# Turning x1 on VectorE and by transfers in place of TensorE, with a new order inside a chunk

## The chip, the cores and the metric

The kernel runs on one core of a Trainium2 chip, alone. The time is device microseconds (us) of one execution. Engines are named as in the profile: PE is TensorE (PEld its weight loads), DVE is VectorE, ACT is ScalarE, POOL is GpSimd, SP is SyncE, which here does nothing but start DMA transfers.

## The reference

A post-norm block of two layers on x of shape (2, 4096, 256), all in float32:

```python
u = x @ W_in + b_in;  g = sigmoid(x @ W_gate + b_gate)
h_t = tanh(h_prev @ A + u_t @ Bm)              # 64 states, over t
y_t = g_t * (h_t @ C.T + u_t @ D.T) + (1 - g_t) * x_t
x1  = layernorm(x + ys @ W_out + b_out + x)
h   = gelu(x1 @ bw1.T + b1)                    # 1024 wide; bw: sign(w) times the row's mean |w|
out = layernorm(x1 + h @ bw2.T + b2)
```

## The kernel before

Time is cut into 64 segments of 64 steps, so that one step of the recurrence handles 128 sequences at once (2 batches of 64 segments). 48 warm-up steps give the first states, then 64 steps follow. The 8192 rows are worked in 16 chunks of 512 rows (`NC`), each held as 4 blocks (`TB`) of 128 rows, or transposed as 2 halves (`KD`) of 128 features by 512 rows. The feed-forward products split their float32 operand into a high part (fp32r, a cast on ACT) and a low part (a subtraction on DVE), and multiply both by the signs of the weights; a scale per row or column comes after.

A chunk goes through these steps; the names are methods of `Chunk`:

- `load`: transfers of states and inputs (hu, L349, two halves TOP and LOW) and of x by rows (xn, L351). `load_x` fetches x transposed (xt, L337).
- `mix`: two state products per chunk into ps_y (L370), POOL adds the bias row to xn (L355), DVE makes d (L377). `mix_end`: L382 and L385, which leaves y in the tile tg.
- `project`, in two halves: y times W_out into ps_z (L395). After the second half the sum x1 (L406) and its statistics (L256 four times, L260 four times, L265), then POOL takes the power (L266).
- `shift` (L271) and `norm` (L279, four instructions on ACT).
- `turn`: eight PE transposes of 128x128 into ps_t (L423), then ACT casts xhi (L431) and DVE subtracts xlo (L433). `rest`: POOL adds the bias row b2 to x1 (L355).
- `up(g)` for g 0 to 3: two groups of four 128x512 products into ps_h (L451), GELU on ACT (L458), cast to hhi (L467). `low(g)`: hlo on DVE (L474). `down(g)`: sixteen products with hhi and hlo into ps_o (L490). After down 3 the `scale` (L506), then `add` (L512) and `stats`, and `store`: normalisation on DVE (L281, four) and the transfer out (L527).
- A recurrence step is two small products (ps_s, L157) and a tanh (L158).
- `gate`: four 128x512 products into ps_g (L313) and a tanh each half (L361).

The order on PE, ACT, DVE and POOL is the order in which the program emits the work (`manual_schedule`, L655). The order of SP's queue was left to a scheduler before. The loop at L723 emits for each c from 0 to 14: up 0 of chunk c, low 0, a recurrence step, down 2 of chunk c-1, the load for c+3, shift and norm of c+1, mix of c+2, up 1, a step, down 3 of c-1, add and statistics of c-1, a gate half (c 1 to 12), the turn of c+1, low 1, rest, up 2, low 2, the store of c-1, a step, down 0, the first half of project for c+2, up 3, a step, down 1, low 3, the second half of project. `emit`'s costs and due times play no part inside that loop, since `since` is set far below zero at L721.

Buffers that matter: ps_y, ps_t and ps_z share one tile of PSUM; ps_o is a single tile; ps_h and ps_g share three banks; h has two buffers, hhi and hlo three, xhi and xlo two, xn four, xt eight, hu three.

## Time and profile before

| | us |
|---|---|
| median of 3 runs | 451.56 |
| the three runs | 451.21 to 453.75 |
| the profiled execution | 451.76 |
| its span in the profile | 450.0 |
| PE busy | 438.2 (97%) |
| DVE busy | 357.4 (79%) |
| ACT busy | 259.9 (58%) |
| POOL busy | 177.6 (39%) |

The profile records one execution, and its own time stands in the table beside the runs. A row of instructions names line, engine, operation and `out<-in` tile names, then busy time and the mean of one in ns. A row of the timeline gives the start in us, the length, and how many instructions were merged (x8). Matmuls overlap in the pipeline, so the length of one is longer than the distance between the starts of two; distances between starts are the better measure. "idle before <-X" says that the engine waited and that X ended the wait. The recurrence and the loading of weights fill the first 90 us; the loop runs from there to about 423 us, and the last chunk's feed-forward part ends the span.

### The profile page before, as it was taken

How to read it: one execution, taken by the hardware profiler on the slowest of the kernel's cores; microseconds unless marked ns; L12 is line 12 of the kernel's file. 1: busy time of each engine (PE TensorE's matmuls, PEld its weight loads, DVE VectorE, ACT ScalarE, POOL GpSimd, SP SyncE). 2: the span in 40 equal slices, each digit the busy share in tenths (PEclk: the TensorE clock that was granted, in tenths of full speed). 3: DMA queues.
4: the chain of work that ended last, by engine and by line, in shares of the span. 5: the costliest groups of instructions: out<-in, count | busy, mean ns of one | idle time of the engine just before them, and what ended most of it. 6: DMA issues, size and time to landing. Idle time of an engine off the chain costs nothing.

```text
span 450.0 us, 6729 instructions
## 1 busy us (share of the span) xinstructions
PE 438.2 (97%) x2506; PEld 355.6 (79%) x2506; DVE 357.4 (79%) x597; ACT 259.9 (58%) x424; POOL 177.6 (39%) x177
## 2 busy tenths in 40 slices
PE   8999999999999999999999999999999999999992
PEld 5665766788888888887979797979788888897982
DVE  0245927967979797989898889899898989887774
ACT  2443541585656574847474747566666656565771
POOL 1001300643545454545445454545454545433413
PEclk9999999999999999999999999999999999999997
DMA  8997824221133313331331313111202020201013
GB/s 298 306 320 289 290 67 134 69 86 23 48 108 104 108 58 106 105 106 58 105 106 61 105 60 105 61 58 50 70 20 87 1 93 1 93 1 48 1 47 101
DMA packets 14838, 44.51 MB, mean 99 GB/s; under 512 B 2000, under 2 KB 3024, under 8 KB 14800
## 3 DMA queue, kind: packets, MB, share of 16 engines
q1 hardware_dynamic: 14224, 43.65, 29.2%
q8 instruction: 22, 0.36, 0.4%
q10 hardware_dynamic: 576, 0.37, 0.3%
q14 instruction: 16, 0.13, 0.1%
HBM read 31.43 MB, written 8.39 MB: 88 GB/s over the span
## 4 chain that ended last, share of the span: by engine, by line
PE 86%; DVE 6%; DMA 3%; ACT 3%; issue 1%; POOL 1%; SPq 0%; POOLq 0%; DVEq 0%
PE ps_h L451 24%; PE ps_o L490 23%; PE ps_z L395 12%; PE ps_g L313 11%; PE ps_y L370 6%; PE ps_s L157 5%; PE ps_u L131 3%; PE ps_t L423 3%; DMA xt<-in_xT 3%; DVE hlo L474 1%; ACT xn L279 1%; ACT h L458 1%; DVE xn L281 1%; DVE bs_a L256 1%; ACT hhi L467 1%
## 5 line engine op out<-in xcount | busy, mean ns | idle before, releaser
L458 ACT ACTIVATE h<-ps_h,bias_c,al 128x512 f32<-128x512 f32 x128 | 97.4, 776 | 86.3 <-PE ps_h L451 80.3
L490 PE MATMUL ps_o<-sg,hhi 128*128 128x256 f32 x496 | 121.3, 285 | 0.0
L490 PE MATMUL ps_o<-sg,hlo 128*128 128x256 f32 x496 | 117.9, 279 | 0.1
L474 DVE TENSOR_TENSOR hlo<-h,hhi 128x1024 fp32r<-128x1024 f32 (+1 forms) x65 | 83.7, 1305 | 23.1 <-ACT hhi L467 23.0
L490 PEld LDWEIGHTS ps_o<-sg,hlo 128*128 128x128 f32 x496 | 93.5, 188 | 1.1 <-DVE hlo L474 0.3
L490 PEld LDWEIGHTS ps_o<-sg,hhi 128*128 128x128 f32 x496 | 93.5, 189 | 0.8
L451 PE MATMUL ps_h<-xhi,sg 128*128 128x512 f32 x256 | 91.8, 440 | 0.0
L355 POOL TENSOR_TENSOR xn<-xn,bo_r 128x256 f32<-128x256 f32 x64 | 65.4, 1052 | 48.4 <-DMA xn<-in_x 48.4
L451 PE MATMUL ps_h<-xlo,sg 128*128 128x512 f32 x256 | 80.1, 394 | 0.2
L355 POOL TENSOR_TENSOR xn<-xn,b_r 128x256 f32<-128x256 f32 x64 | 70.8, 1134 | 2.0 <-PE ps_t L423 2.0
L467 ACT CAST hhi<-h 128x1024 fp32r<-128x1024 f32 (+1 forms) x65 | 67.3, 1037 | 2.0
L313 PE MATMUL ps_g<-xt,w_gate 128*128 128x384 f32 (+3 forms) x208 | 66.3, 430 | 0.2 <-DMA xt<-in_xT 0.2
L266 POOL TENSOR_TENSOR rs_a<-rs_a,neg_half 128x4 f32<-128x4 f32 x16 | 17.2, 1075 | 121.3 <-DVE rs_a L265 96.6
L395 PE MATMUL ps_z<-w_out,tg 128*128 128x256 f32 x256 | 60.7, 380 | 0.0
L158 ACT ACTIVATE st<-ps_s 64x128 f32<-64x128 f32 x112 | 30.1, 269 | 47.6 <-PE ps_s L157 47.1
L451 PEld LDWEIGHTS ps_h<-xlo,sg 128*128 128x128 f32 x256 | 48.1, 188 | 11.8 <-DVE xlo L433 0.9
L451 PEld LDWEIGHTS ps_h<-xhi,sg 128*128 128x128 f32 x256 | 46.6, 189 | 13.4 <-issue 6.2
L157 PEld LDWEIGHTS ps_s<-st,wab 128*128 128x128 f32 x224 | 38.5, 188 | 22.2 <-ACT st L158 10.0
L266 POOL TENSOR_TENSOR rs_b<-rs_b,neg_half 128x4 f32<-128x4 f32 (+1 forms) x17 | 19.2, 1132 | 87.9 <-PE ps_s L157 49.9
L395 PEld LDWEIGHTS ps_z<-w_out,tg 128*128 128x128 f32 x256 | 46.1, 189 | 5.1
L279 ACT ACTIVATE xn<-xn,nm_a,rs_a 128x256 f32<-128x256 f32 x60 | 31.2, 591 | 26.5 <-DVE nm_a L271 26.5
L157 PE MATMUL ps_s<-st,wab 128*128 128x128 f32 x224 | 43.9, 278 | 0.1
(73 smaller groups left out, 483.5 us busy)
## 6 DMA issues: line engine op xcount, KB each, us to landing
xt<-in_xT SPq DMA_DIRECT2D x35, 512.0 KB, 4.2
xn<-in_x SPq DMA_DIRECT2D x16, 512.0 KB, 3.4
out_y<-xn SPq DMA_DIRECT2D x15, 512.0 KB, 2.6
hu<-st SPq DMA_DIRECT2D x32, 128.0 KB, 2.2
w1t<-in_w1T SPq DMA_DIRECT2D x2, 512.0 KB, 5.6
w1n<-in_w SPq DMA_DIRECT2D x2, 512.0 KB, 6.3
w2t<-in_w2T SPq DMA_DIRECT2D x2, 512.0 KB, 4.7
xt<-in_xT SPq DMA_DIRECT2D x2, 256.0 KB, 3.4
```

Of the source, the lines that this page charges most:

```text
L157: nc.tensor.matmul(p_h, ab, st[:, j].rearrange("p b k -> p (b k)"), start=True, stop=True)
L158: nc.scalar.activation(h_of[:, j + 1].rearrange("p b k -> p (b k)"), p_h[TOP, :], AF.Tanh)
L266: nc.gpsimd.tensor_tensor(rs, rs, neg_half[:, cut], ALU.pow)
L279: nc.scalar.activation(r, r, AF.Identity, bias=self.sh[:, i : i + 1], scale=rs)
L313: nc.tensor.matmul(ps[:, cut], w_gate[:, k, bass.ts(m, P)], xt_[:, k, cut], start=k == 0 and i == 0, stop=k == KD - 1, skip_group_check=True,)
L355: nc.gpsimd.tensor_tensor(r[:, i, :], r[:, i, :], row, ALU.add)
L395: nc.tensor.matmul(self.ps_z[:, i, :], self.y[:, k, bass.ts(i, P)], w_out[:, k, :], start=k == 0, stop=k == KD - 1,)
L451: nc.tensor.matmul(ps, sg1[:, k, bass.ts(j, P)], part[:, k, :], start=n == 0, stop=n == 2 * KD - 1,)
L458: nc.scalar.activation(h[:, i, :], ps, AF.Gelu, bias=b1_c[:, j : j + 1], scale=al1[:, j : j + 1],)
L467: nc.scalar.copy(hi[:, part, :], h[:, part, :])
L474: nc.vector.tensor_sub(lo[:, i, :], h[:, i, :], hi[:, i, :].bitcast(FP))
L490: nc.tensor.matmul(ps[:, i, :], part[:, j % 2, bass.ts(tb, P)], sg2[:, j, :], start=j == 0 and part is self.h[j // 2][0] and first, stop=j ...
```

## The change

For chunks 2 to 14 (`far`), x1 is no longer turned by PE. `blocks` transposes it on DVE in one instruction, 32x32 blocks at a time, into xb; sixteen transfers per chunk, each of 32 partitions by two runs of 512 bytes, then carry the blocks within SBUF to the right partitions, straight into the tile of xlo. `split` casts xhi from there on ACT and subtracts on DVE. The columns of the result stand in another order of rows inside a chunk, (a, i, c) in place of (i, a, c); the GELU undoes it as it writes h. `split` is emitted inside up 3, between its two groups.

Inside a chunk the order changes: shift and norm of c+1, low 3 of c-1 and `blocks` come first; low 0 comes after the mix; both halves of project stand ahead of up 3; the sum x1 and its statistics are made half by half. The store's normalisation moves from DVE to ACT (which needs a shift on DVE) and stands after the cast of up 2. SP's queue now has the order in which the program emits its transfers, and the load of xn is split from that of hu (`load_n`) and comes after the store. d shares the tile of o. In the last chunk of the loop, low 3 follows up 0 of chunk 15.

```diff
-    with tc.manual_schedule(engines={ET.PE, ET.Activation, ET.DVE, ET.Pool}):
+    with tc.manual_schedule(engines={ET.PE, ET.Activation, ET.DVE, ET.Pool, ET.SP}):
...
-            self.d = wk.tile([P, KD, N], FP, tag="y", name=f"d{nm}", bufs=1)
+            self.d = wk.tile([P, KD, N], FP, tag="o", name=f"d{nm}", bufs=1)
...
+            if half == 0:
+                self.x1 = self.xn
+                self.st1 = Stats(self.x1, f"a{nm}")
+            blocks = range(half * TB // 2, last + 1)
+            cut = slice(blocks[0], last + 1)
+            x1 = self.x1[:, cut, :]
+            nc.vector.scalar_tensor_tensor(
+                x1, x1, 2.0, self.ps_z[:, cut, :], ALU.mult, ALU.add
+            )
+            self.st1.gather(blocks)
             if half == 1:
-                x1 = self.x1 = self.xn
-                nc.vector.scalar_tensor_tensor(x1, self.xn, 2.0, self.ps_z, ALU.mult, ALU.add)
-                self.st1 = all_stats(x1, f"a{nm}")
+                self.st1.merge(range(TB))
+                self.st1.root(range(TB))
...
+        def blocks(self):
+            nm, Q = self.nm, P // 32
+            xb = wk.tile([P, DM // 32, TB, 32], FP, tag="xb", name=f"xb{nm}", bufs=1)
+            nc.vector.transpose(
+                out=xb, in_=self.x1.rearrange("p i (b r) -> p b i r", r=32)
+            )
+            self.lo = wk.tile([P, KD, N], FR, tag="xlo", name=f"xlo{nm}")
+            for a in range(Q):
+                for q in range(Q):
+                    nc.sync.dma_start(
+                        out=self.lo.bitcast(FP)[bass.ts(q, 32), :, bass.ts(a, P)],
+                        in_=xb[bass.ts(a, 32), q :: Q, :, :].rearrange("p k i c -> p k (i c)"),
+                    )
+            yield
+
+        def split(self):
+            self.hi = wk.tile([P, KD, N], FR, tag="xhi", name=f"xhi{self.nm}")
+            nc.scalar.copy(self.hi, self.lo.bitcast(FP))
+            nc.vector.tensor_sub(self.lo, self.lo.bitcast(FP), self.hi.bitcast(FP))
+            self.h = {}
+            self.far = True
...
                 nc.scalar.activation(
-                    h[:, i, :],
-                    ps,
+                    to,
+                    ps.rearrange("p (a i c) -> p a i c", a=P // 32, c=32) if self.far else ps,
...
+                if i == 0 and between is not None:
+                    between()
...
         for c in range(end):
+            far = 0 < c < end - 1
+            if c > 0:
+                do(c + 1, "shift")
+                do(c + 1, "norm")
+                do(c - 1, "low", 3)
+                if far:
+                    do(c + 1, "blocks")
+            do(c, "up", 0)
+            step()
+            do(c - 1, "down", 2)
+            if c > 0:
+                do(c + 2, "mix")
+                do(c + 2, "mix_end")
+            do(c, "low", 0)
+            do(c + 3, "load")
             do(c + 6, "load_x")
             if c % 2 == 0:
                 do(10 + c // 2, "load_gate_x")
-            do(c, "up", 0)
-            do(c, "low", 0)
-            step()
-            do(c - 1, "down", 2)
-            do(c + 3, "load")
-            if c > 0:
-                do(c + 1, "shift")
-                do(c + 1, "norm")
-                do(c + 2, "mix")
-                do(c + 2, "mix_end")
...
-            do(c + 1, "turn")
+            if not far:
+                do(c + 1, "turn")
...
             do(c, "up", 2)
+            if c < end - 1:
+                do(c - 1, "store", range(TB), nc.scalar)
+                do(c + 3, "load_n")
             do(c, "low", 2)
             if c == end - 1:
                 do(c - 1, "stats")
-            else:
-                do(c - 1, "store")
...
             do(c + 2, "project", 0)
-            do(c, "up", 3)
+            do(c + 2, "project", 1)
+            do(c, "up", 3, False, ch[c + 1].split if far else None)
             step()
             do(c, "down", 1)
-            do(c, "low", 3)
...
-            do(c + 2, "project", 1)
...
         do(end, "up", 0)
+        do(end - 1, "low", 3)
         do(end, "low", 0)
```

More of the change, by code (lines that the diff above doesn't have):

```diff
@@ L333, in __init__ @@
             self.c, self.nm, self.at, self.xt = c, name, at, None
+            self.far = False
         def load_x(self):
@@ L349, in load, with load_n @@
                 nc.sync.dma_start(out=self.hu[r, :], in_=src.rearrange("p j b k -> p (j b k)"))
+        def load_n(self):
+            c, nm = self.c, self.nm
             self.xn = xp.tile([P, TB, DM], FP, tag="xn", name=f"xn{nm}", bufs=4)
@@ L440, in rest, with up @@
             yield
-        def up(self, g, apart=False):
+        def up(self, g, apart=False, between=None):
             nm = f"{self.nm}_{g}"
@@ L457, in up @@
                     )
+                to = h[:, i, :]
+                if self.far:
+                    to = to.rearrange("p (i a c) -> p a i c", a=P // 32, c=32)
                 nc.scalar.activation(
-                    h[:, i, :],
-                    ps,
+                    to,
+                    ps.rearrange("p (a i c) -> p a i c", a=P // 32, c=32) if self.far else ps,
                     AF.Gelu,
@@ L587, in redo @@
             self.load()
+            self.load_n()
             pieces = [self.gate, self.mix, self.mix_end, lambda: self.project(0), lambda: self.project(1)]
@@ L643, in do @@
             ch[i].load()
-        elif what in ("load_x", "load_gate_x"):
+        elif what in ("load_n", "load_x", "load_gate_x"):
             getattr(ch[i], what)()
@@ L679, in gated_recurrence_then_binary_ffn @@
                 load_xT(n + 3)
+                for i in ((0,), (1, 2))[n - 5]:
+                    ch[i].load_n()
             for i in range(7 - before):
```

## The prediction, made before the run

> **What bounds the kernel now.** I read the busy line and the chain of waits first, then the windows, then TensorE's own lines around one turn.

> ```profile
> PE 438.2 (97%) x2506; PEld 355.6 (79%) x2506; DVE 357.4 (79%) x597; ACT 259.9 (58%) x424; POOL 177.6 (39%) x177
> ...
> PE 86%; DVE 6%; DMA 3%; ACT 3%; issue 1%; POOL 1%; SPq 0%; POOLq 0%; DVEq 0%
> ```

> TensorE is 97% busy and 86% of the chain. A busy share can hide gaps, so the next view is a window of one chunk (23.41 us: the sums at L406 start at 104.80, 128.21, 151.61 and so on), and the two windows of chunks 13 and 14.

> ```profile
> 196.00:219.40 23.40, 23.40 (x138) 19.64 (x138) 20.94 (x34) 14.58 (x23) 11.29 (x10) 1.00 0.24 79
> ...
> 384.00:404.80 20.80, 20.80 (x125) 18.05 (x124) 18.54 (x32) 13.12 (x17) 9.19 (x9) 1.00 0.10 32
> 404.80:422.60 17.80, 16.91 (x109) 14.59 (x107) 13.41 (x27) 12.63 (x17) 7.18 (x8) 1.00 0.08 31
> ```

> The columns are length, then PE, PEld, DVE, ACT, POOL. In the loop PE never pauses, so work taken off PE shortens the chunk. But DVE is at 20.94 of 23.40: only 2.5 us looser. That is the next bound, and most of what follows is about it.

> What a turn costs PE is seen by comparing two places that differ only in it. Weight loads, in order:

> ```profile
> 202.02 0.30 PEld L370 LDWEIGHTS ps_y<-hu,cd 128*128 128x128 f32 x2
> ...
> 205.46 0.41 PEld L157 LDWEIGHTS ps_s<-st,wab 128*128 128x128 f32 x2
> 207.63 0.30 PEld L313 LDWEIGHTS ps_g<-xt,w_gate 128*128 128x128 f32 x2
> ...
> 209.03 0.14 PEld L423 LDWEIGHTS ps_t<-ident,xn 128*128 128x128 f32 x1 [0.24 <-issue]
> ...
> 211.95 0.19 PEld L157 LDWEIGHTS ps_s<-st,wab 128*128 128x128 f32 x1
> ```

> Four 128x512 products (ps_y) and an up group take 205.46 - 202.02 = 3.44 us. Four products of the same shape (ps_g), the turn and an up group take 211.95 - 207.63 = 4.32. The turn is the difference, 0.88 us; I use 0.87. The L423 row's mean of 273 ns would give 2.2 us for eight, which is wrong for pipelined matmuls.

> [...] L385 takes 1.65 us with GpSimd adding and 1.23 at 71.08 without; L474 pairs take 2.88 in place of 2.3.

> **The change, part by part.**

> Turns: 13 of 16 leave PE (chunks 2 to 14). With nothing else late: 23.41 - 0.87 = 22.54 us per chunk. Merging the projection halves saves PE nothing: the same products remain.

> DVE per chunk: minus four L281 (2.65 us, now ACT); plus the block transpose ([...]I take 1.2, like L377), plus a shift L271 (0.16 alone, 0.73 with GpSimd), plus about 0.2 for halving L406. Net about -0.6: 20.3 of 22.54.

> DVE's order decides. Its chain begins with the state product:

> ```profile
> 200.07 0.38 PE L157 MATMUL ps_s<-st,wab 128*128 128x128 f32 x2
> ...
> 203.31 0.69 DVE L271 SCALAR_TENSOR_TENSOR nm_a<-mv_a,rs_a 128x4 f32<-128x4 f32 x1
> 204.04 1.22 DVE L377 TENSOR_TENSOR d<-ps_y,xt 128x1024 f32<-128x1024 f32 x1
> ```

> The up group before 200.07 takes 1.84, so the chunk begins at 198.23 and d at +5.81. Then, start to start: d 1.26, L382 1.26, L385 1.25 (GpSimd should be done), hlo0 1.14, scale 1.25, add 1.25, four statistics 1.33, merge 0.40, 0.07, hlo1 1.14, shift 0.73 (GpSimd has just begun), hlo2 1.42 (1.14 to 1.69), two half sums 0.71 each (0.61 to 0.75), their statistics 0.66 each, 0.48, xlo 1.14: 16.86 us, ending at 22.67. The next chunk's first xlo product is 0.46 after its start, so this loop needs 22.21 us and PE 22.54. PE still sets the pace, by 0.33 us. Bounds: 1.05 less with all low ends; 1.43 more if L382 is 1.76 (seen at 252.12), L385 1.65, hlo2 1.69, xlo 1.4: 23.64, no gain.

> Transpose wait: it needs norm on ACT, which ends about 3.0 (last cast at 0.9, then 2.08). Behind it on DVE is d at 5.81[...]; past 2.8 it costs one for one.

> ACT: four applications (2.08) come in. 14.58 + 2.08 = 16.7 of 22.54. They wait for the shift at about 16.5 and end at 18.6; the next GELU is due at 19.7. The GELU's reordered write has no row; bounds 0 and 0.3 us each. 0.3 delays the casts by 0.6 and eats the cover. I take 0. The xhi copy waits for all sixteen transfers; behind it are a GELU, its cast, the norm.

> SP: sixteen transfers per chunk, in order, ahead of the hu and xt loads.

> ```profile
> 63.66 1.13 SPq L349 DMA_DIRECT2D hu<-st  x2
> ...
> 67.92 1.13 SPq L349 DMA_DIRECT2D hu<-st  x2
> ```
> ```profile
> hu<-st SPq DMA_DIRECT2D x32, 128.0 KB, 2.2
> ```

> SBUF-to-SBUF issues run at 0.64 us start to start (1.13 - 0.49) and land in 2.2. From 4.2: 4.2 + 16 x 0.64 + 2.2 = 16.6. The xhi copy wants them at 20.5, so 3.9 us is spare; hu and xt then issue by 16, a chunk ahead of use. Bounds per issue: 0.43 and 1.29 (longest L351). Limit: (20.5 - 4.2 - 2.2)/16 = 0.88. out_y now waits for ACT, lands near 22, xn (3.4) at 25.5; GpSimd's bias add takes it 3 us into the next chunk, needed at 18. Covered.

> Steps that change places. The norm comes before the up group 0 and hlo3 of the chunk before behind it: hlo3 ends near 2.0 and its product (down 3) starts at 7.6. hlo0 now comes after L385, ending at 10.7; it frees the h buffer for the GELUs of up 2 (12.3) and feeds down 0 (13.2). The scale after it ends at 12.0; it empties ps_o, the only buffer, for the same down 0. GpSimd's order (power, bias add, power, bias add) stays. Each of these has a microsecond or more to spare; if DVE runs later than I say they are next after xlo. On SP, hu and xt loads move behind the sixteen, the xn load behind the store's landing, as before. The instruction order of the changed kernel has the eight transposes in three chunks only, so it does what it says.

> Head: hu halves are now issued together, behind the later of their inputs. Before, only the TOP half came at 67.92, where PE waits; its partner follows by 0.57. Cost 0.6, on the path.

> Chunks 11 and 12 have no recurrence steps: PE 22.70 - 0.87 = 21.83, DVE loop 22.07: gain 0.6 each. Chunk 13 has no gate product: PE 20.0, but there the statistics stand directly ahead of the shift, which then waits for GpSimd's power (1.15), and two compare steps (0.55) enter: 5.67 + 18.56 - 0.46 = 23.8 against 20.88: a loss of 2.9. Chunk 14's turn, still on PE, no longer waits for norm, which is now first:

> ```profile
> PEld ps_t L423 <- ACT xn L279: 1.7, 4, 0.6
> ```

> That returns 1.7.

> Sum: chunks 1 to 10, 8.7; 11 and 12, 1.3; 13 and 14, -1.2; head -0.6: 8.2 us off. The profiled execution has 451.76 (span 450.0 and 1.76 around it): 443.6, or 443.4 beside the median 451.56. What is left out, above all nine waits ahead of one xlo instruction, can only cost: I take **444.0**.

> **Rivals.** (1) DVE's loop sets the pace: GpSimd collides more, or the waits cost 0.3 each. For it: 0.33 us of cover. Against: two rows moved away from GpSimd. At 22.9 per chunk 0.5 x 10 = 5.0 stays, chunks 11 and 12 give 0.6, 13 and 14 cost 1.5, the head 0.6: 3.5 off, 448. At the upper bounds nothing stays: 454. (2) Slower: SP. Mechanism: sixteen small issues in one queue. Decides from 0.88 us per issue; at 1.0 the last lands at 4.2 + 16 + 2.2 = 22.4, xhi is 1.9 late in 13 chunks, 24.7 on top of 443.4: 468. For it: pieces of two rows per partition have no row, and 1.29 occurs. Against: 0.64 seen. (3) Everything is hidden, with DVE at its low ends, chunk 13 too: 8.7 + 1.7 + 1.7 - 0.6 = 11.5 off: 440.

> **Chances.** Forecast 0.52; (1) 0.28, of which a third within 0.5%; (2) and other slower ends of it 0.14; (3) 0.06. Measurement tells about 0.5% (2.3 us) from no change. Faster by more 0.75, within 0.1, slower 0.15. The forecast's own range is 441.5 to 446.5; for 8 in 10 it reaches through (1): 440.5 to 451.5.

> **What would show it.** Right: L406 halves 22.5 us apart, PE full in the loop, xhi not waiting on DMA, sixteen issues in some 10 us. Wrong: PE waiting for xlo behind a full DVE (1), or ACT's xhi waiting for the transfers (2). Chunk 13 should be longer than 20.88, and the turn of chunk 15 without a wait.

## The result and the profile after

| | before | changed |
|---|---|---|
| median of four runs, us | 451.85 | 503.4 |
| range, us | 451.21 to 453.75 | 502.2 to 503.82 |
| span of the profiled execution, us | 450.0 | 501.5 |
| mean granted TensorE clock | 0.994 | 0.954 |

The ratio is 1.113, with a 95% interval of 1.109 to 1.117. The change costs 51.5 us where 8 were forecast as a gain. The three lines of the page that answer to those of before (busy time, granted clock by slice, chain by engine), for the changed kernel:

```profile
PE 450.4 (90%) x2402; PEld 358.0 (71%) x2402; DVE 341.9 (68%) x587; ACT 285.6 (57%) x476; POOL 178.6 (36%) x177
...
PEclk9999999999898989899898999898989899998998
...
PE 56%; DVE 28%; issue 6%; POOL 5%; DMA 2%; ACT 1%; SPq 0%; POOLq 0%; DVEq 0%
```

TensorE fell from 97% to 90% busy, and its busy time *rose* by 12 us though 104 instructions were taken off it. The clock line says why that is no contradiction: the digits fall to 8 in the loop, and the same work is busy longer there. The first two products of up 3 (L488) take 1.21 us in chunk 6 (265.42 to 266.63, clock 0.50) and 0.64 in chunk 7 (292.03 to 292.67, clock 1.00). And TensorE's share of the chain fell from 86% to 56%, with VectorE up from 6% to 28%: TensorE now waits. For what, TensorE's own list of waits in the changed kernel tells (total us, times, longest):

```profile
PE ps_z L399 <- DVE xn L414: 39.1, 16, 5.4
PE ps_y L374 <- DMA hu<-st: 1.6, 2, 1.3
```

Nothing like the first line stood in the kernel before. In all 16 chunks the products of project wait for L414, VectorE's new sum x1. The timeline of one chunk shows the place. First TensorE (start, length, in square brackets the idle time before and what ended it):

```profile
258.97 1.89 PE L399 MATMUL ps_z<-w_out,tg 128*128 128x256 f32 x8
263.38 2.60 PE L399 MATMUL ps_z<-w_out,tg 128*128 128x256 f32 x8 [2.52 <-DVE xn L414]
265.42 1.41 PE L488 MATMUL ps_h<-xhi,sg 128*128 128x512 f32 x2
266.63 1.05 PE L488 MATMUL ps_h<-xlo,sg 128*128 128x512 f32 x2
```

The first half of project starts at 258.97 and is followed by nothing until 263.38: 2.52 us of pause, in the middle of project. Then VectorE in the same stretch:

```profile
258.79 1.22 DVE L516 TENSOR_TENSOR hlo<-h,hhi 128x1024 fp32r<-128x1024 f32 x1
260.91 0.68 DVE L271 SCALAR_TENSOR_TENSOR nm_b<-mv_b,rs_b 128x4 f32<-128x4 f32 x1 [0.91 <-POOL rs_b L266]
261.52 1.21 DVE L516 TENSOR_TENSOR hlo<-h,hhi 128x1024 fp32r<-128x1024 f32 x1
262.65 0.68 DVE L414 SCALAR_TENSOR_TENSOR xn<-xn,ps_z 128x512 f32<-128x512 f32 x1
...
266.02 0.69 DVE L414 SCALAR_TENSOR_TENSOR xn<-xn,ps_z 128x512 f32<-128x512 f32 x1 [1.91 <-PE ps_z L399]
```

The sum of the first half (L414 at 262.65) could have started when the first half was done at 260.86. It stands behind the shift of the store (L271), which waits 0.91 us for GpSimd's power, and behind low 2. It ends at 263.33, and TensorE goes on at 263.38. Thereupon the second sum waits for TensorE (1.91 us): the two halves of project and the two sums have become a chain that goes to and fro.

The pause is not the whole loss. The windows of the same stretch (length, then PE, PEld, DVE, ACT, POOL, then the granted clock, DMA share and GB/s):

```profile
258.97:260.86 1.89, 1.89 (x10) 1.33 (x8) 1.03 (x1) 0.01 (x1) 1.84 (x2) 1.00 0.29 66
260.86:263.38 2.52, 0.00 (x0) 0.00 (x1) 2.43 (x4) 1.75 (x4) 2.52 (x4) 1.00 0.95 258
263.38:265.42 2.04, 2.04 (x8) 1.74 (x9) 0.73 (x2) 0.49 (x2) 1.30 (x2) 0.81 1.03 422
265.42:266.63 1.21, 1.21 (x4) 0.94 (x3) 0.61 (x1) 0.00 (x0) 0.00 (x0) 0.50 0.54 220
266.63:267.49 0.86, 0.86 (x4) 0.66 (x2) 0.83 (x4) 0.00 (x0) 0.00 (x0) 0.50 0.00 0
267.49:268.67 1.18, 1.18 (x6) 0.95 (x4) 0.46 (x6) 0.94 (x2) 0.55 (x1) 0.77 0.63 142
268.67:270.77 2.10, 2.10 (x19) 2.10 (x18) 1.29 (x2) 2.07 (x3) 0.95 (x2) 1.00 0.44 174
243.78:270.77 26.99, 24.47 (x130) 19.97 (x129) 19.64 (x35) 16.75 (x27) 11.03 (x11) 0.94 0.35 108
```

Some 1.3 us after the pause the granted clock falls to 0.50 and stays there for 3.4 us. The clock shares of the four windows after the pause come to 2.04 x 0.19 + (1.21 + 0.86) x 0.50 + 1.18 x 0.23 = 1.69 us of lost time. Pause and low clock make 4.2 of the 4.5 us by which this chunk (26.99) exceeds the 22.5 that TensorE's work takes (shown below by two kernels).

Over the whole trace these are 39.1 us of pauses and twelve times 3.41 us at half clock, some 20 us lost. Together that is more than the 51.5, since TensorE has thirteen turns less to do. By stage, from the start of up 0 of each chunk in the four traces, in us:

| stage | before | changed | e1, single sum | e12, last version |
|---|---|---|---|---|
| up to chunk 0 | 87.24 | 90.42 | 87.96 | 86.95 |
| chunk 0 | 17.17 | 18.31 | 17.43 | 17.43 |
| chunks 1 to 10 | 234.15 | 268.55 | 230.93 | 225.07 |
| chunks 11, 12 | 45.40 | 51.34 | 45.22 | 43.38 |
| chunks 13, 14 | 38.62 | 45.20 | 43.05 | 37.07 |
| the rest | 27.40 | 27.70 | 28.00 | 28.07 |
| span | 450.0 | 501.5 | 452.6 | 438.0 |

### The profile page after: what moved, and what is told of

Same layout as the page of the kernel before. It is cut to its first block, busy times and chain, and to the rows that moved or that the text cites. A ratio compares the mean times of both kernels' runs of the same rounds, so it can differ in the third digit from the quotient of the medians.

```text
span 501.5 us, 6854 instructions
## 1 busy us (share of the span) xinstructions
PE 450.4 (90%) x2402; PEld 358.0 (71%) x2402; DVE 341.9 (68%) x587; ACT 285.6 (57%) x476; POOL 178.6 (36%) x177
## 2 busy tenths in 40 slices
DMA packets 31479, 51.34 MB, mean 102 GB/s; under 512 B 5328, under 2 KB 19664, under 8 KB 31440
## 4 chain that ended last, share of the span: by engine, by line
PE 56%; DVE 28%; issue 6%; POOL 5%; DMA 2%; ACT 1%; SPq 0%; POOLq 0%; DVEq 0%
PE ps_h L488 15%; PE ps_o L532 13%; PE ps_z L399 10%; PE ps_g L313 6%; PE ps_y L374 5%; POOL rs_b L266 5%; DVE bs_b L256 4%; PE ps_s L157 4%; DVE hlo L516 4%; DVE d L386 3%; DVE d L381 3%; DVE o L548 3%; DVE tg L389 3%; DVE xn L554 3%; PE ps_u L131 3%
## 5 line engine op out<-in xcount | busy, mean ns | idle before, releaser
L498 ACT ACTIVATE h<-ps_h,bias_c,al 128x512 f32<-128x512 f32 x128 | 97.5, 777 | 90.1 <-PE ps_h L488 84.7
L399 PE MATMUL ps_z<-w_out,tg 128*128 128x256 f32 x256 | 76.4, 451 | 39.1 <-DVE xn L414 39.1
L488 PE MATMUL ps_h<-xhi,sg 128*128 128x512 f32 x256 | 98.6, 468 | 0.0
L399 PEld LDWEIGHTS ps_z<-w_out,tg 128*128 128x128 f32 x256 | 54.2, 222 | 53.1 <-DVE xn L414 45.1
L359 POOL TENSOR_TENSOR xn<-xn,bo_r 128x256 f32<-128x256 f32 x64 | 68.5, 1101 | 53.0 <-DVE negb L195 47.8
L516 DVE TENSOR_TENSOR hlo<-h,hhi 128x1024 fp32r<-128x1024 f32 (+1 forms) x65 | 79.7, 1228 | 6.3 <-ACT hhi L509 6.1
L266 POOL TENSOR_TENSOR rs_b<-rs_b,neg_half 128x4 f32<-128x4 f32 (+1 forms) x17 | 27.3, 1606 | 157.8 <-DVE rs_b L265 157.6
L488 PE MATMUL ps_h<-xlo,sg 128*128 128x512 f32 x256 | 82.1, 402 | 0.1
L313 PE MATMUL ps_g<-xt,w_gate 128*128 128x384 f32 (+3 forms) x208 | 66.1, 430 | 0.1
L488 PEld LDWEIGHTS ps_h<-xhi,sg 128*128 128x128 f32 x256 | 50.3, 203 | 20.1 <-issue 12.0
L359 POOL TENSOR_TENSOR xn<-xn,b_r 128x256 f32<-128x256 f32 x64 | 60.4, 973 | 2.9 <-PE ps_t L436 2.9
L488 PEld LDWEIGHTS ps_h<-xlo,sg 128*128 128x128 f32 x256 | 49.9, 195 | 12.7 <-DVE xlo L446 0.7
L157 PEld LDWEIGHTS ps_s<-st,wab 128*128 128x128 f32 x224 | 38.6, 189 | 22.0 <-ACT st L158 9.0
L279 ACT ACTIVATE xn<-xn,nm_b,rs_b 128x256 f32<-128x256 f32 x58 | 30.2, 590 | 40.1 <-DVE nm_b L271 40.1
L414 DVE SCALAR_TENSOR_TENSOR xn<-xn,ps_z 128x512 f32<-128x512 f32 x32 | 21.8, 682 | 35.1 <-PE ps_z L399 35.1
## 6 DMA issues: line engine op xcount, KB each, us to landing
hu<-st SPq DMA_DIRECT2D x32, 128.0 KB, 2.3
```

Source lines behind the costliest of these rows:

```text
L157: nc.tensor.matmul(p_h, ab, st[:, j].rearrange("p b k -> p (b k)"), start=True, stop=True)
L266: nc.gpsimd.tensor_tensor(rs, rs, neg_half[:, cut], ALU.pow)
L279: nc.scalar.activation(r, r, AF.Identity, bias=self.sh[:, i : i + 1], scale=rs)
L313: nc.tensor.matmul(ps[:, cut], w_gate[:, k, bass.ts(m, P)], xt_[:, k, cut], start=k == 0 and i == 0, stop=k == KD - 1, skip_group_check=True,)
L359: nc.gpsimd.tensor_tensor(r[:, i, :], r[:, i, :], row, ALU.add)
L399: nc.tensor.matmul(self.ps_z[:, i, :], self.y[:, k, bass.ts(i, P)], w_out[:, k, :], start=k == 0, stop=k == KD - 1,)
```

## The experiments

Theory A: the wait at ps_z, and the low clock that the pause brings, make the loss. Rival B: VectorE's loop or the transfers fill the chunk anyway, and the wait would only move. Rival C: the low clock is a cause of its own. Rival D: halving the sum costs wherever it stands. `...` marks lines left out of an edit. Times are medians; "before" ran beside each.

**e1, the sum in one piece.** The changed kernel with the old sum:

```diff
-            if half == 0:
-                self.x1 = self.xn
-                self.st1 = Stats(self.x1, f"a{nm}")
-            blocks = range(half * TB // 2, last + 1)
...
             if half == 1:
-                self.st1.merge(range(TB))
-                self.st1.root(range(TB))
+                x1 = self.x1 = self.xn
+                nc.vector.scalar_tensor_tensor(x1, self.xn, 2.0, self.ps_z, ALU.mult, ALU.add)
+                self.st1 = all_stats(x1, f"a{nm}")
```

> The changed kernel with the sum x1 and its four statistics made once, after the second half of project, as in the kernel before; everything else of the change stays. Theory A (TensorE's second half of ps_z waits for VectorE's sum of the first half, 2.5 us a chunk, and the clock granted after that pause costs some 1.6 us more): both go, a chunk falls from 27.0 to 22.5 to 23.0 us, the time to 444 (441 to 452). Rival B (VectorE's loop or the transfers are what fills the chunk, and the wait at ps_z only takes the place of a wait for xlo): the pause moves to the first xlo product, the time stays above 485. Rival C (the low clock is a cause of its own, from load or heat, and would come without the pause): the pause goes, the clock stays near 0.95, the time is 465 to 480.

Measured: 454.9 us, ratio to before 1.007 (1.005 to 1.009), clock 0.992. So 48.5 of the 51.5 us were the halved sum in this place: A holds, B and C fall as explanations of the big loss. But it misses 444 by 11 us and is still slightly slower than before. TensorE's waits now name another releaser, and VectorE's timeline shows the loop:

```profile
PE ps_h L479 <- DVE xlo L461: 8.2, 13, 2.7
```

```profile
203.71 1.23 DVE L381 TENSOR_TENSOR d<-ps_y,xt 128x1024 f32<-128x1024 f32 x1 [2.10 <-PE ps_y L374]
...
214.94 0.68 DVE L271 SCALAR_TENSOR_TENSOR nm_b<-mv_b,rs_b 128x4 f32<-128x4 f32 x1 [0.91 <-POOL rs_b L266]
215.55 1.21 DVE L507 TENSOR_TENSOR hlo<-h,hhi 128x1024 fp32r<-128x1024 f32 x1
216.68 1.21 DVE L410 SCALAR_TENSOR_TENSOR xn<-xn,ps_z 128x1024 f32<-128x1024 f32 x1
217.93 1.41 DVE L256 BATCH_NORM_STATS2 bs_a<-xn 128x6 f32<-128x256 f32 x4
...
220.05 1.22 DVE L461 TENSOR_TENSOR xlo<-xlo,xhi 128x1024 fp32r<-128x1024 f32 x1 [0.23 <-issue]
```

From d at 203.71 to the end of xlo at 221.27 it is 17.56 us; from there TensorE needs 5.6 us (up 0, a step, down 2, ps_y) until it can release the next d. That is 23.13 us, the chunk measured. Chunk 1, which doesn't wait for xlo yet, takes 22.51. So the prediction's first rival was there, hidden behind the larger loss.

**e8, both half sums behind both halves.** To part the halving from its place:

```diff
-            blocks = range(half * TB // 2, last + 1)
-            cut = slice(blocks[0], last + 1)
...
             if half == 1:
+                for blocks in (range(0, TB // 2), range(TB // 2, TB)):
+                    cut = slice(blocks[0], blocks[-1] + 1)
...
```

> The changed kernel with the sum still in halves, but both halves emitted behind the products of both halves of project. Only the place of the first half sum differs from the changed kernel. Theory A (the place makes the wait): no pause at ps_z, as the single sum within 2 us: 455 (453 to 457). If halving the sum costs by itself (rival D): stays above 480.

Measured: 457.7 us, ratio 1.012 (1.009 to 1.015); no wait for L414's sum on TensorE. The instructions are those of the changed kernel, and 45.7 us are gone. D falls; what the halves cost by themselves is the 2.8 us to e1 (a chunk 23.33 in place of 23.13).

**e3, the pause filled.** Idle products between the halves; the wait stays, the pause doesn't:

```diff
+FILL = 5
...
+        def fill(c):
+            ps = p_1.tile([P, N], FP, tag="h", name=f"ps_f{c}")
+            for _ in range(FILL):
+                nc.tensor.matmul(ps[:, :DM], ident, w_out[:, 0, :], start=True, stop=True)
...
             do(c + 2, "project", 0)
+            fill(c)
             do(c + 2, "project", 1)
```

> The changed kernel with five idle products of 128x256 on TensorE between the halves of project, into a PSUM buffer that is free and that nobody reads: work of 2.4 us in the pause of 2.5 us. The wait stays, only the pause doesn't. Theory A with the low clock as a consequence of the pause: up 3 after it runs at full clock, 1.5 us less per chunk, some 25 us in 16 chunks: 478 (472 to 486), mean clock 0.99. Rival C (the clock falls from load or heat): no gain or a loss, 503 to 515, clock 0.95 or less.

Measured: 488.4 us, ratio 1.079 (1.073 to 1.085), clock 0.995. TensorE's timeline and, after it, the window from up 3 to the next up 0, whose clock is the third figure from the end:

```profile
252.78 2.32 PE L773 MATMUL ps_f<-w_out,ident 128*128 128x256 f32 x10
255.45 1.99 PE L400 MATMUL ps_z<-w_out,tg 128*128 128x256 f32 x8 [0.35 <-DVE xn L415]
257.10 0.81 PE L489 MATMUL ps_h<-xhi,sg 128*128 128x512 f32 x2
```

```profile
257.10:261.24 4.14, 4.14 (x29) 3.77 (x28) 2.97 (x9) 2.80 (x4) 1.02 (x1) 1.00 0.32 111
```

ps_f is the filling. The wait is 0.35 us now, up 3 runs at full clock, and a chunk takes 25.3 instead of 27.0. More work made the kernel 15 us faster: the low clock is a consequence of the pause, and C falls. I had expected 25 us. It acts in some eleven chunks rather than 16, and in chunks 0 and 14 the filling is longer than the pause, or there is none (1.1 and 2.3 us more).

**e2, the halves of project apart again**, as in the kernel before, the sum in halves:

```diff
             do(c + 2, "project", 0)
-            do(c + 2, "project", 1)
             do(c, "up", 3, False, ch[c + 1].split if far else None)
             step()
             do(c, "down", 1)
+            do(c + 2, "project", 1)
```

> The changed kernel with the second half of project back behind down 1; the sum stays in halves. Theory A: the half sum on VectorE has up 3, a step and down 1 (4 us of TensorE) to be done in, more than the 2.5 us of the wait, so the pause goes: 445 (442 to 452). The second sum and its statistics end some 4 us later, ahead of the next shift. Rival B: over 485. Rival C: 465 to 480. If halving the sum costs by itself wherever it stands (rival D): about 503, as changed.

Measured: 479.6 us, ratio 1.059 (1.052 to 1.065). A miss by 35 us, though the wait at ps_z is down from 39.1 to 3.7 us. Two lines of all engines' waits show what came in its place:

```profile
ACT xn L279 <- DVE nm_a L271: 57.0, 14, 5.6
...
PE ps_s L157 <- ACT st L158: 20.4, 20, 2.1
```

The statistics now end so late that ScalarE, whose next instruction is the norm, stands 4 us per chunk for its shift. Behind the norm stand GELU and the tanh of a recurrence step, and TensorE's next step product waits for that tanh. The norm at the head of a chunk needs the sum early, and with the halves of project apart it comes late; so in this order the merged project is needed.

**e4, the kernel before with the halved sum alone**, in the words of the change:

```diff
+            if half == 0:
+                self.x1 = self.xn
+                self.st1 = Stats(self.x1, f"a{nm}")
+            blocks = range(half * TB // 2, last + 1)
...
             if half == 1:
-                x1 = self.x1 = self.xn
-                nc.vector.scalar_tensor_tensor(x1, self.xn, 2.0, self.ps_z, ALU.mult, ALU.add)
-                self.st1 = all_stats(x1, f"a{nm}")
+                self.st1.merge(range(TB))
+                self.st1.root(range(TB))
```

> The kernel before with one part of the change alone: the sum x1 and its statistics in halves. There the halves of project lie 4 us apart (up 3, a step and down 1 between them). Theory A: the second half finds the sum of the first done, no pause at ps_z, 451.5 (450 to 453.5). Rival D (halving costs by itself): each chunk pays 2 us or more, 480 and above.

Measured: 458.7 us, ratio 1.012 (1.006 to 1.018). The loop's chunks are unchanged (23.41), as A has it. Nearly all of the 7 us lies in two places that the expectation left out, the head and chunk 13:

```profile
PE ps_z L395 <- DVE xn L410: 6.1, 4, 3.9
```

Chunk 13 goes from 20.88 to 26.64 (3.9 us of that wait, then the low clock, a mean of 0.59 over the next 6 us: there VectorE has other work queued ahead of the half sum), and the head loses 2.2.

**e11, the merged project alone**, on the kernel before, with the single sum:

```diff
             do(c + 2, "project", 0)
+            do(c + 2, "project", 1)
             do(c, "up", 3)
...
-            do(c + 2, "project", 1)
```

> The kernel before with one part alone: both halves of project ahead of up 3, the sum in one piece. The prediction said that this saves TensorE nothing; the order of the change with the turn on TensorE had 23.74 us a chunk in place of 23.41, of which up 2 to up 0 of the next has 0.45 more. If merging itself costs that: 0.3 to 0.45 in each of ten to twelve chunks, 455 to 457. If the 0.33 came from the other moves of the order: 451 to 452.5.

Measured: 451.9 us, ratio 1.000 (0.998 to 1.002), a chunk 23.43. Merging costs TensorE nothing (0.02 us a chunk) and saves nothing.

**e7 and e10, the new order with the turn on TensorE.** In e7 on top of e1, in e10 on top of e9, which comes below (there the shift and norm keep their places under another name).

```diff
-            far = 0 < c < end - 1
+            far = False
```

> The kernel of the single sum with every chunk turned on TensorE: the new order of a chunk, the store on ScalarE and the queue in order, but no block transposes, no transfers and no reordered write of GELU. If the turn costs TensorE 0.87 us and the rest of the change nothing there: a chunk is 22.5 + 0.87 = 23.4 us, as before, and the time 452 (450 to 456). If the transposition by VectorE and transfers is what holds the single sum's kernel at 454.9 (rival): it is faster than that one, below 450.

Measured: 460.3 us, ratio 1.016 (1.009 to 1.022), so 8 us more than expected and 5.4 more than e1. A chunk takes 23.74; chunk 14 takes 20.69 in place of 17.74, where the norm ahead of GELU makes TensorE stand 3.0 us and the low clock follows (mean 0.72 over the next 6 us). In this form the order by itself is a loss, and the transposition pays for part of it (e1).

> The kernel of e9 with every chunk turned on TensorE, no block transposes and no transfers: what the turn itself is worth in the mended order. Measured so far: the stretch from up 1 to up 2 is 6.80 us with a turn and 5.60 without, so 1.2 us per chunk with a gate product, and 0.8 without: thirteen chunks 15 us, 455 (452 to 457). If the turn costs TensorE 0.87 us, as the prediction had it: 451 to 452. If the order alone does the work (rival): below 445.

Measured: 460.5 us, ratio 1.019 (1.015 to 1.022). This too is 5 us above what I expected. The waits of TensorE in e10:

```profile
PE ps_z L399 <- DVE xlo L439: 4.1, 7, 1.2
PE ps_y L374 <- DMA hu<-st: 2.4, 1, 2.4
```

ps_t and ps_z share one buffer, and xlo, which empties ps_t, now comes late for ps_z. So this isn't a clean price of the turn. The cleaner one is the chunk of e11 (turn on TensorE) against that of e12 below: in chunks 1 to 10 TensorE doesn't wait in either and has the same products otherwise. 23.43 - 22.51 = 0.92 us.

**e5, xhi and xlo earlier.** On top of e1, against VectorE's loop:

```diff
             do(c, "up", 2)
+            if far:
+                ch[c + 1].split_hi()
+            do(c, "low", 2)
             if c < end - 1:
                 do(c - 1, "store", range(TB), nc.scalar)
                 do(c + 3, "load_n")
-            do(c, "low", 2)
...
-            do(c + 2, "project", 1)
-            do(c, "up", 3, False, ch[c + 1].split if far else None)
+            do(c + 2, "project", 1, p_m, "m", ch[c + 1].split_lo if far else None)
+            do(c, "up", 3)
```

Here `split_hi` is the cast, `split_lo` the subtraction, which project issues between the sum and its statistics.

> The kernel of the single sum (454.9 us) with a new order around xlo: on ScalarE the xhi cast stands ahead of the store's normalisation, where ScalarE waits 2.6 us for the shift anyway; on VectorE low 2 stands ahead of that shift, and xlo directly behind the sum, ahead of its statistics. If what is left of the loss there is VectorE's loop from d to xlo (17.5 us, then 5.6 us on TensorE until the next d, 23.1 in all): xlo ends 3 us earlier, TensorE's 0.6 us wait per chunk goes, a chunk is 22.5 us, chunk 14 doesn't wait for xlo: 446 (443 to 449). If it is the transfers (sixteen issues of 0.68 us and the landing) that come too late: ScalarE now waits for them ahead of the normalisation and of the GELU of up 3, and the time is 455 or more.

Measured: 447.6 us, ratio 0.989 (0.982 to 0.995). Of TensorE's thirteen waits for xlo one of 0.4 us is left, in chunk 14. A chunk takes 22.50 to 23.46; what varies is the stretch from up 3 to up 0 (4.08 to 5.04). Two of its waits:

```profile
ACT xhi L462 <- DMA xlo<-xb: 30.8, 13, 4.0
...
PEld ps_s L157 <- ACT st L158: 14.0, 35, 1.1
```

ScalarE now stands 2.4 us per chunk for the transfers. That in itself is free (in e12 it is 35.0 us in all, and TensorE is full); but the tanh of the step after up 2 stands behind it, and the next step's product waits for it.

**e6, the ends.** On top of e5: the LOW half of hu is issued ahead of the TOP half, the norm of chunk 15 comes after up 0 of chunk 14, and the comparison of states moves into chunk 14.

```diff
-                (TOP, h_of[:, bass.ds(c * SPC + 1, SPC)]),
                 (LOW, u_of[:, bass.ds(c * SPC, SPC)]),
+                (TOP, h_of[:, bass.ds(c * SPC + 1, SPC)]),
...
-            if c > 0:
+            if far:
                 do(c + 1, "shift")
                 do(c + 1, "norm")
+            if c > 0:
                 do(c - 1, "low", 3)
...
+            if c == end - 1:
+                do(c + 1, "shift")
+                do(c + 1, "norm")
+                for _ in parts_met:
+                    pass
```

> The kernel of e5 with the ends mended too: the LOW half of hu is issued ahead of the TOP half (0.6 us in the head), the norm of chunk 15 comes after up 0 of chunk 14 as in the kernel before, and the comparison of states is made in chunk 14, where VectorE is idle. Beside e5: 0.6 in the head, up to 3 in chunks 13 and 14: 442 (439 to 446). If the ends were not to blame, as e5 within 1 us.

Measured: 443.9 us, ratio 0.979 (0.973 to 0.986). The head is 1.4 us shorter than in e5, and chunk 14 goes from 18.25 to 15.78. The edits were not run apart; the two numbers tell the head from the end, but not the norm from the comparison.

**e9 and e12, the step ahead of xhi.** e9 also puts low 0 ahead of d; e12 doesn't.

```diff
             do(c, "up", 2)
+            if c < end - 2:
+                step()
             if far:
                 ch[c + 1].split_hi()
...
-            step()
             do(c, "down", 0)
```

and in e9 alone:

```diff
+            do(c, "low", 0)
             if c > 0:
                 do(c + 2, "mix")
                 do(c + 2, "mix_end")
-            do(c, "low", 0)
```

> The kernel of e6 with two places more: the recurrence step after up 2 is issued ahead of the xhi cast on ScalarE (its tanh stood behind xhi, which waits 2.4 us for the transfers, and behind the normalisation, so the next step's product waited), and low 0 stands ahead of d on VectorE. If the spread of e6's chunks (22.55 to 23.4 us) is that tanh: every chunk of the loop 22.5 us, 3 to 4 us in ten chunks, and up to 1.2 at the scale in chunk 13: 440 (438 to 442). If it is the transfers holding ScalarE ahead of the GELU of up 3 (rival): as e6, 443 to 445.

Measured: 445.2 us, ratio 0.984 (0.982 to 0.987): no gain on e6. From up 3 to up 0 it is 4.1 us in every chunk, as expected; but from up 2 to up 3 it is up to 8.15 in chunks 1 to 10, in place of 7.56, and 11.09 in chunk 13, where the longest of these waits is followed by the low clock (mean 0.72 over the next 6 us):

```profile
PE ps_o L527 <- DVE o L543: 3.9, 4, 2.2
```

low 0 ahead of d pushes the scale back, and down 0 needs the buffer that the scale empties. One of the two moves was right and one wrong, which e12 parts:

> The kernel of e6 with the recurrence step ahead of the xhi cast alone; low 0 stays behind the mix (in e9 it stood ahead of d, and the scale behind it came late for TensorE). If both readings hold: the stretch from up 3 to the next up 0 is 4.1 us in every chunk as in e9, and the one from up 2 to up 3 7.56 us as in e6; ten chunks of 22.5 us, 4.3 us less than e6's: 439.6 (438 to 441.5). If the losses of e9 came from the step's new place and not from low 0: 443 to 446.

Measured: 440.3 us, ratio 0.972 (0.969 to 0.975), the fastest of all. Its busy and clock lines, the one wait of TensorE that is left in the loop (in chunk 13), and a chunk:

```profile
PE 426.2 (97%) x2402; PEld 344.9 (79%) x2402; DVE 337.1 (77%) x571; ACT 283.5 (65%) x476; POOL 158.6 (36%) x177
...
PEclk9999999999999999999999999999999999999997
```

```profile
PE ps_o L527 <- DVE o L543: 1.0, 1, 1.0
```

```profile
196.00:218.50 22.50, 22.50 (x129) 18.84 (x128) 19.45 (x32) 16.33 (x26) 8.77 (x11) 1.00 0.37 106
```

TensorE is 22.50 of 22.50 us busy at clock 1.00, and chunks 1 to 10 take 22.50 or 22.51 each.

## Why the prediction was wrong

**The step that failed** is the entry "two half sums 0.71 each": in the prediction it is time on VectorE and nothing else, and the forecast of 22.54 us a chunk, "With nothing else late", puts TensorE's wait for the first half sum at nothing, without a reason. That wait is 2.5 us in chunk 6, 39.1 us in all, and the low clock after most of these waits costs 1.7 us more. "Merging the projection halves saves PE nothing: the same products remain" is true of the products (e11), but it is the merging that leaves no time for the first half sum. Who is released by that sum was not asked. It is TensorE's own second half, since both halves and both sums share the tile ps_z. The program says so before any run. These are TensorE's instructions of the project of chunk 15, with what each waits for; the kernel before has no wait in the middle:

```
L399 Matmult ps_z15<-w_out,tg15 128x256 x4
L399 Matmult ps_z15<-w_out,tg15 128x256 [waits DVE]
L399 Matmult ps_z15<-w_out,tg15 128x256 x3
```

The size was nearly at hand too. The prediction's chain has the first half sum start 12.50 us after d, so at 5.81 + 12.50, and end at 19.02; in the changed kernel the first half of project ends at 17.08 of its chunk and the sum at 19.55. So the forecast order of VectorE, set against the end of the first half, contained 1.9 of the 2.5 us. None of the rivals named this wait either; the slower end was given to the queue of SP. What no figure of the prediction contained is the clock after the pause, 1.7 us in most chunks.

**Right, with the size:** TensorE's part. 22.54 us a chunk was forecast, and 22.51 is what chunk 1 of e1 and ten chunks of e12 take; the turn was put at 0.87 and is 0.92. The block transpose takes 1.25 us, the mean of 13 at L455 in the changed kernel (taken: 1.2, an estimate from L377's 1.22). GELU's reordered write shows no cost: 777 ns, the mean of 128 at L498, against 776 at L458 before. SP's issues in the changed kernel's timeline, and their row on its page:

```profile
247.99 11.31 SPq L461 DMA_DIRECT2D xlo<-xb  x16
```

```profile
xlo<-xb SPq DMA_DIRECT2D x208, 32.0 KB, 1.9
```

The first line is one chunk's sixteen issues on SP, the second the size of one and its median landing. Sixteen in 11.31 us are 0.71 each (forecast 0.64, limit 0.88), and they land in 1.9 us (2.2). Rival (2) is refuted.

**Mis-sized:** VectorE's loop. Forecast 22.21, measured 23.13 in e1. The chain from d to xlo is 17.56 in place of 16.86, and TensorE's part 5.6 in place of 5.35. The term that was missing is the shift's wait for GpSimd's power ahead of low 2, 0.91 us; the prediction counted the shift's own 0.73 alone. low 2 took 1.13 rather than 1.42, which hid part of it. With 0.33 us of cover, this alone brings rival (1) in, even without the wait at ps_z, as e1 shows. In e12 the loop is no bound, since xlo goes ahead of the statistics.

**The ends.** The head's 0.6 was right (0.7 in e1), and e6 removes it. Chunk 13 costs 1.7 in e1 (forecast 2.9). Chunk 14 was to return 1.7 and loses 2.7: TensorE stands 2.7 us for xlo, and the clock falls (0.72 over the next 6 us). That the norm stands ahead of GELU there had been counted as a gain for the turn, not as a hold-up for ScalarE (e7). In e12 the two chunks together return 1.6.

**Still open:** whether the second half would wait if the two halves of ps_z were separate tiles. The wait is one that the program asks for; no run shows whether the hardware needs it. ps_y and ps_t use the same tile and would have to be divided too, and it was not tried. Of the remainder of e1 to e12, 14.6 us, each part went with one of three runs (7.3 in e5, 3.7 in e6, 3.6 in e12).

## What to carry to other kernels

When a read of an accumulator is split so that it can start earlier, look at which later write of the same tile stands behind it in program order: that writer now waits for the reader's engine and for all that is queued ahead there (here 2.52 us in chunk 6, 39.1 in all). Read the list of each engine with its waits, not only its order, and set the moment when each releaser is due against the moment when it is wanted. A reordering is best judged by its smallest parts: of the moves made here one cost 48 us, and the rest, with the order of e5, e6 and e12, gain 2.8%.

## What was not expected of the hardware

The length of the pause alone does not decide here: 2.85 us were followed by the low clock and 2.87 were not. In the changed kernel's clock record the stretches at 0.50 begin at 128.09, 155.40, 182.71, 210.01, 237.32, 264.63, 315.83, 343.13, 370.44, 397.75 and 448.95 us. All the distances from one to the next are 8, 14 or 15 times 3.413 us, though the chunks are 27.0 us long; each stretch lasts 3.41 us, the last one twice that (one more lies at the end, where TensorE has no work left). So I laid windows of 3.413 us over the trace, so that they end where such stretches begin, and counted TensorE's idle time in each. Here are two windows of the changed kernel, each with the one that follows it; the first pair is chunk 6, the second chunk 7 (length, PE, PEld, DVE, ACT, POOL, clock, DMA share, GB/s):

```profile
261.21:264.63 3.42, 1.25 (x6) 1.12 (x7) 2.87 (x5) 2.24 (x5) 3.42 (x4) 1.00 0.99 325
264.63:268.04 3.41, 3.41 (x10) 2.66 (x9) 1.89 (x8) 0.31 (x1) 0.05 (x1) 0.50 0.51 186
288.52:291.93 3.41, 1.54 (x7) 1.39 (x8) 2.56 (x5) 2.24 (x5) 3.17 (x4) 1.00 0.46 175
291.93:295.35 3.42, 3.42 (x23) 3.03 (x22) 2.15 (x9) 2.01 (x3) 0.83 (x1) 1.00 0.55 180
```

The first window has 2.17 us of idle time, and the next is at half clock. The pause of chunk 7 is as long (2.53 us), but an edge at 288.52 divides it, 1.87 us fall in one window, and the clock stays. From 60 us to 12 us before the end, the changed kernel's trace has 112 such windows at full clock: all 11 with 2.17 us or more of idle time were followed by one at half clock, and none of the 101 with 1.87 or less was. The kernel before, with edges laid from the half clock at its own end (444.69 us), has 110, with at most 0.73 us of idle time, and none was. The other pause that was spared, in chunk 12 (2.87 us), is divided as that of chunk 7 is (1.45 and 1.42 us). So in this trace a pause of some 2.5 us was followed by a loss of about 1.7 us more (1.69 in chunk 6) where 2.17 us or more of it fell in one window, and by none where an edge divided it: chunk 7 of the changed kernel takes 25.39 us, its neighbours 27.0, without any edit. What sets the edges was not shown. The way back to full clock was not the same each time: ten of the eleven stretches lasted one window, with at most 0.24 us of idle time in it; the one after the longest pause, 5.43 us, lasted two, with 0.69 us of idle time in the first.
